# Four due times moved in a step loop over 64 chunks: sums of v, kb, an accumulating transfer, and T2 against KV

## The chip, the cores and the metric

The kernel runs on one core of a Trainium2 chip, in float32 throughout. The metric is the device time of one execution in microseconds (us); for a kernel that was run several times it is the median.

The engines are named as the profile names them: PE is TensorE (PEld its weight loads), DVE is VectorE, ACT is ScalarE, POOL is GpSimd, and SP is SyncE, which here only issues DMA transfers. GpSimd issues some transfers as well. Each engine works through its own list of instructions in order and waits on semaphores of the others.

## The reference

Input x has 8 images of 512 channels with 64 x 64 points. Two attention layers follow one another.

```
layer 0:  f = Wf x + bf                      (64 channels, 4096 points)
          g = maxpool2x2(Wg x + bg)          (64 channels, 1024 points)
          v = maxpool2x2(Wh x + bh)          (256 channels, 1024 points)
          beta = softmax(f^T g) over the 1024 points
          x = gamma * (Wv (v beta^T) + bv) + x
layer 1:  Q, K, V = wq x + bq, wk x + bk, wv x + bv      (64, 64, 512 channels)
          Qf, Kf = 10 relu(.) + exp(10 min(., 0))
          KV   = Kf V^T                                   (64 x 512)
          norm = 1 / (Qf . (sum of Kf over the points + eps))
          x = x + gamma * Qf KV * norm
```

## The kernel before, in words

An image is cut into 8 chunks of 512 points, so there are 64 chunks. The function `step(s)` is called for s from -9 to 64 and lays out what belongs to one step; j = s mod 8 is the place of chunk s in its image. A step with 0 <= s < 55 does four things side by side:

- For chunk a = s + 9 it makes f, g and v (`a_conv`). Three by four blocks of weights times four by two of x are multiplied in 20 products in place of 24, which asks for sums of blocks of x (GpSimd, tiles `v`, line 360) and for sums of the products' chains A to E out of PSUM (VectorE, tiles `h` and `fg`, line 377 and its neighbours). f goes through HBM and comes back later (`store_f`, `load_f`); v is pooled, turned and moved through HBM into `vT` (`flip_v`, `move_v`, `join_v`).
- For chunk s + 1 it makes the scores and their exponentials (`weigh`, tile `E`: TensorE `s`, line 616, ScalarE line 620), adds the exponentials over the 1024 points on VectorE (`sum_of_e`, tile `r`, lines 654 to 659), has TensorE finish these sums (`total`, tile `tot`, line 673), takes the reciprocals (line 683), spreads them over the partitions through HBM (`spread_inverses`: transfers `rd`, line 688, and `rb`, line 690), and multiplies E by them in four blocks (`normalize_block`, line 713).
- For chunk s it multiplies v with the normalized E (`attend`) and the result with Wv (`project`), each in seven products in place of eight. This asks for four sums of blocks of v (`sums_of_v`, tiles S1 to S4, once an image, lines 597 to 601), four sums of blocks of E (`sums_of_e`, tiles T1 to T4, lines 720 to 729) and sums behind the products. In `project` the results are added to x: either ScalarE copies a result out of PSUM and GpSimd adds it (`evict`, lines 812 and 815; `add_copy`, lines 823 and 824), or VectorE adds it from PSUM (`add`, line 818). Then x goes to HBM as the input of layer 1, its features are taken (`features`, tile `pk`, line 858), and it is turned (`flip_x`, `across`, `along`) so that K's features can be multiplied with it (`gather`, tile `pg`, summed in `G`).
- For the image before, b - 1, it finishes layer 1. In the step with j = 0, `start_kb` makes ksum and the matrix `kb` from the sums of K's features (lines 973 to 980, seven small VectorE operations), `normalize` multiplies Q's features with kb (`pd`, line 1067), inverts (line 1074) and spreads the result (`rn`), and `turn_G` turns G. In the step with j = 1, `make_KV` makes KV: TensorE `pkv` (line 1036), VectorE out of PSUM into `kv` (lines 1045 and 1049). In the steps with odd j, `finish` multiplies Q's features of a pair of chunks with KV (`pa`, line 1105), ScalarE copies the result to `y` (line 1108), and GpSimd issues two transfers of 1 MB each that add y onto the output in HBM (line 1111).

The order is written out by hand. Inside a step, `at(t, fn, ...)` puts an operation on a list with a due time t; the list is sorted by t, and the instructions are issued in this order. A due time is thus no time of the clock: it says only behind which other operations an instruction stands in its engine's list. VectorE, GpSimd, ScalarE, TensorE and SP each get their part of the one list.

Tiles are scarce. E, r, T1 to T4, S1 to S4 and `xb` have one buffer each, `y` has two, which are also used for the weights w_v1, and PSUM has eight banks. In a step with 0 <= s < 55 the banks of s, pa and pkv are taken in turn out of five (m3 to m7); most others are fixed.

The second half of the program repeats all of this with safer exponentials (`general=True`); it is only entered when a sum left the range, which does not happen with these inputs.

The lines that place what is changed (of the kernel before):

```python
if a % NCHUNK == 0:
    at(29.25 if early else 31.3, sums_of_v, (a - 1) // NCHUNK)
...
at(5.7 if a < TOTAL else 0.2, start_kb, b_c)
...
finish(pair, (2, 3), at, 32.4 if cover else t + 0.1, None if cover else 22.7 if a >= TOTAL else 8.206)
```

Of the kernel before, what the change touches and what calls it, by code (L numbers as in the profile page):

```python
# [8 lines left out]
F32 = mybir.dt.float32  # L9
AF = mybir.ActivationFunctionType  # L10
ALU = mybir.AluOpType
# [4 lines left out]
P = 128  # L16
# [6 lines left out]
def tile_two_attention_blocks(  # L23
# [21 lines left out]
    nc = tc.nc  # L45
# [6 lines left out]
    NCHUNK = N // CH  # L52
# [129 lines left out]
    def run(ctx, general):  # L182
# [402 lines left out]
                vT[:, 0:CV].rearrange("p (v q i) -> p v q i", v=VT, q=NT),  # L585
            )

        def sums_of_v(b):

            hm = MT // 2  # L590
            a11, a12, a21, a22 = (
                st[b]["vT"][:, bass.ts(j, hm), bass.ts(i, P)] for i in range(2) for j in range(2)
            )
            s1, s2, s3, s4 = (
                work1.tile([P, hm, P], F32, tag=f"S{i}", name=f"S{i}_{b}") for i in range(1, 5)
            )
            nc.gpsimd.tensor_tensor(s1, a21, a22, ALU.add)
            nc.gpsimd.tensor_tensor(s4, a11, a12, ALU.add)
            nc.gpsimd.tensor_tensor(s4, s1, s4, ALU.subtract)
            nc.gpsimd.tensor_tensor(s2, a11, s1, ALU.subtract)  # L600
            nc.gpsimd.tensor_tensor(s3, a11, a21, ALU.subtract)
            st[b]["v7"] = {1: a11, 2: a12, 3: s4, 4: a22, 5: s1, 6: s2, 7: s3}


# [175 lines left out]
        def project(s, at, t, t_store):  # L780
# [62 lines left out]
            at(t + t_evict[1], evict, (1, 1))  # L843
            at(t + (3.8 if last else 6.5), add, (0, 0), 2, ALU.add)
            at(t + t_add[0], add, (1, 0), 7, ALU.add)
            more = add if last else add_copy
            at(t + (t_add[1] if last else 3.41), more, (1, 0), 4, ALU.subtract)
            at(t + t_add[2], more, (1, 1), 7, ALU.add)
            at(t + t_add[3], add_rest)
            if s < TOTAL - 1:  # L850
                at(t_store, store)
# [363 lines left out]
        def step(s):  # L1215
# [10 lines left out]
            def at(t, fn, *args):  # L1226
                work.append((t, len(work), fn, args))
# [12 lines left out]
            if here:  # L1240
                ts = {
                    1: (0.0, None), 2: (1.7, 4.0), 3: (3.45, None), 6: (8.8, 10.7), 7: (10.5, 12.4),
                    4: (12.2, 14.1), 5: (13.85, 17.7),
                } if a <= TOTAL else {
                    1: (0.0, None), 2: (1.7, 4.0), 3: (3.9, None), 6: (14.4, 16.1), 7: (16.2, 17.9),
                    4: (17.9, 19.7), 5: (19.6, 22.5),
                }
                if s == 0:
                    ts.update({6: (4.0, 4.5), 7: (4.1, 4.6), 4: (4.2, 4.7), 5: (4.3, 4.8)})
                attend(s, at, ts)  # L1250
                if not (a <= TOTAL and s):
                    at(-0.6, sums_of_e, s, 3)
                at(5.6 if a <= TOTAL and s else 0.3, sums_of_e, s, 4)
                if a <= TOTAL and s:
                    at(-0.1, sums_of_e, s, 2)
            if 0 <= s - 1 < TOTAL:
                late_k = waits(s - 1)
                if late_k:
# [23 lines left out]
                if here:  # L1282
                    gather(s - 1, at, *((30.9, 32.6) if late_k else (14.3, 16.6) if a <= TOTAL else (12.6, 13.5)))
            if c_here and here and j == 0:
                at(5.7 if a < TOTAL else 0.2, start_kb, b_c)
                if a < TOTAL:
                    turn_G(b_c, at, (18.65, 18.75, 36.5))
                else:
                    turn_G_now(b_c, at, 19.5)
                if a >= TOTAL:  # L1290
                    make_KV(b_c, at, 21.4, 24.2, 24.2)
# [2 lines left out]
            if c_here and here and j == 1 and a <= TOTAL:  # L1294
                make_KV(b_c, at, 5.5, 5.55, 6.0)
            if c_here and here and j == 0:
                normalize(pair, at, 14.2 if a < TOTAL else 12.65, 15.95 if a < TOTAL else 13.7, 35.9 if a < TOTAL else 38.6)
            if c_here and here and j % 2 == 1 and j < NCHUNK - 1:
                normalize(pair + 1, at, 14.2 if a <= TOTAL else 12.65, 15.95 if a < TOTAL else 22.6 if a <= TOTAL else 13.7, 35.9 if a < TOTAL else 38.6)
            if c_here and here and j % 2 == 1:  # L1300

                cover = a == TOTAL
                t = 21.4 if cover else 9.2 if a > TOTAL else 8.0 if j == 1 else 3.6
                finish(pair, (0, 1), at, t, 24.9 if cover else 22.6 if a >= TOTAL else 8.15 if j == 1 else 3.75)
                finish(pair, (2, 3), at, 32.4 if cover else t + 0.1, None if cover else 22.7 if a >= TOTAL else 8.206)
            if 0 <= a < TOTAL:
                if a + 2 < LEAD - 1:
                    a_conv(a + 2)
# [13 lines left out]
            if 0 <= a - 1 < TOTAL:  # L1322
                early = a == NCHUNK
                if early:
                    at(29.2, a_turn, a - 1)
                else:
                    if ("pool", a - 1) in late:
                        at(6.9, late["pool", a - 1])
                    at(18.5 if not here else 6.95, flip_v, a - 1)
                    at(18.7 if not here else 7.0, move_v, a - 1)  # L1330
                    at(20.0 if not here else 22.0 if a % NCHUNK == 0 else 29.0, join_v, a - 1)
                if a % NCHUNK == 0:
                    at(29.25 if early else 31.3, sums_of_v, (a - 1) // NCHUNK)
            if s == -2:
                at(34.3, weigh_two, 0, 0)
                at(34.4, weigh_two, 0, 2)
# [3 lines left out]
            if after:  # L1340
# [25 lines left out]
                if not general:  # L1366
                    at(19.0 if t_invert == 15.9 and a < TOTAL else 26.0 if t_invert > 22 else 21.5, look, n)
                ts = {0: (28.3, 28.29, 33.5, 33.52), 1: (29.35, 29.4, 31.7, 31.8)}
                for i, t in zip((1, 0, 3, 2), ts.get(n, (36.6, 24.72, 29.2, 27.0) if a < TOTAL and c_here and j % 2 else (36.6, 24.0, 29.2, 25.2) if a < TOTAL else (24.3, 26.0, 27.3, 29.2))):
                    at(t, normalize_block, n, i // 2, i % 2)  # L1370
                at(36.606 if a < TOTAL and n else 33.6, sums_of_e, n, 1)
                if a < TOTAL and n:
# [144 lines left out]
```

## Time and profile before

| | |
|---|---|
| median of 3 runs | 2653.46 us (2651.44 to 2654.77) |
| the profiled execution, own time | 2651.42 us |
| its span, first to last instruction | 2649.6 us |
| PE, DVE, ACT, POOL busy | 97%, 81%, 55%, 53% |
| mean granted TensorE clock | 0.993 |
| DMA | 385.86 MB, 146 GB/s in the mean |

A step begins, in all that follows, with its first matmul of `M<-E,vT`; step 16 so begins at 736.25 us of the span and step 11 at 537.85. Steps 2 to 54 repeat in a pattern of eight. Those with even j other than 0 take 36.73 us in most cases; those with odd j take longer, since `pa` and `pd` come on top; the one with j = 1 has KV as well.

How to read the lines: a timeline's line has the start and the duration in us, the engine, the line of the kernel, the operation, output <- inputs with their shapes, the count, and in square brackets how long the engine stood idle before it and what released it. A line of the waits has the waiting instruction, what it waited for, then the total in us, the number of times and the longest. "PEclk" is the share of full speed that TensorE's clock was granted.

### The profile page before, as it was taken

The page shows a single profiled execution, that of the slowest core. Times are in us where ns is not written, and L with a number is a line of the kernel's source. Part 1 is how long each engine was busy: PE and PEld are TensorE (multiplying, and loading weights), DVE is VectorE, ACT ScalarE, POOL GpSimd, SP SyncE. Part 2 cuts the span into 40 slices and gives each one's busy share as a digit, 9 for nine tenths or more (in the row PEclk, how much of TensorE's full clock was granted, in tenths as well). Part 3 has the DMA queues.
Part 4 walks back from the last instruction along what each step waited for, and adds up shares of the span by engine and source line. Part 5 has one row for each costly group of instructions (what it writes and reads, how often), then busy time and mean ns, then how long its engine had stood idle before and what let it go on. Part 6 is the DMA issues. An engine that isn't in the chain of part 4 may idle for free.

```text
span 2649.6 us, 36263 instructions
## 1 busy us (share of the span) xinstructions
PE 2560.7 (97%) x11439; PEld 1847.3 (70%) x11439; DVE 2134.4 (81%) x3271; ACT 1456.1 (55%) x3300; POOL 1403.7 (53%) x1289
## 2 busy tenths in 40 slices
PE   9899999999999999999999999999999999989997
PEld 6677776777767777677776677677776677756664
DVE  6788888787788787888787887877887877878884
ACT  2255654665655665655655655656655556545553
POOL 5646556556556557556556556555556465421112
PEclk9999999999999999999999999999999999999999
DMA  6233443564554554644555545655545555444557
GB/s 181 80 102 118 140 135 121 153 169 131 152 158 128 159 164 129 173 129 137 164 145 156 156 124 140 181 138 157 149 124 165 151 149 154 126 125 126 139 138 261
DMA packets 271711, 385.86 MB, mean 146 GB/s; under 512 B 93404, under 2 KB 111768, under 8 KB 271512
## 3 DMA queue, kind: packets, MB, share of 16 engines
q1 hardware_dynamic: 254264, 323.94, 39.1%
q0 software_dynamic: 15232, 58.72, 11.6%
q8 instruction: 94, 1.54, 0.2%
q10 hardware_dynamic: 2016, 0.79, 0.1%
q14 instruction: 105, 0.86, 0.1%
HBM read 198.71 MB, written 150.04 MB: 132 GB/s over the span
## 4 chain that ended last, share of the span: by engine, by line
PE 72%; DVE 17%; issue 3%; SPq 3%; DMA 2%; ACT 1%; POOL 0%; DVEq 0%; ACTq 0%; POOLq 0%
PE M L741 24%; PE N L802 11%; PE s L616 7%; PE pk L858 6%; PE A L367 5%; PE pg L944 4%; PE pa L1105 4%; DVE E L713 3%; PE B L367 3%; SPq L1015 2%; PE C L367 2%; PE E L367 2%; DVE xf L907 2%; DVE h L377 1%; PE D L367 1%
## 5 line engine op out<-in xcount | busy, mean ns | idle before, releaser
L360 POOL TENSOR_TENSOR v<-xa 128x256 f32<-128x256 f32 x345 | 349.2, 1029 | 496.6 <-DMA xa<-in_x_dram 446.1
L815 POOL TENSOR_TENSOR xb<-xb,n 128x512 f32<-128x512 f32 x192 | 290.7, 1514 | 294.8 <-ACT n L812 294.0
L741 PE MATMUL M<-T,S 128*128 128x256 f32 x1536 | 359.0, 384 | 0.0
L360 POOL TENSOR_TENSOR v<-xa,v 128x256 f32<-128x256 f32 x410 | 346.5, 846 | 18.3
L741 PEld LDWEIGHTS M<-T,S 128*128 128x128 f32 x1536 | 287.1, 190 | 84.5 <-issue 31.7
L542 ACT COPY xT<-xf 32x512 f32<-32x512 f32 x504 | 310.1, 615 | 15.2 <-DVE xf L907 9.3
L713 DVE TENSOR_TENSOR E<-E,rb 128x1024 f32<-128x1024 f32 x220 | 310.4, 1412 | 0.0
L620 ACT ACTIVATE E<-s 128x512 f32<-128x512 f32 x512 | 263.4, 640 | 65.4 <-PE s L616 36.5
L616 PE MATMUL s<-f,g 64*128 64x512 f32 x1024 | 264.6, 621 | 10.7 <-DVE kv L1045 5.7
L1111 POOL DMA_DIRECT2D out_dram<-y x56 | 69.9, 1248 | 358.2 <-ACT y L1108 356.7
L802 PE MATMUL N<-to,w_v 128*128 128x256 f32 x1024 | 253.5, 382 | 4.6 <-ACT n L812 4.5
L741 PE MATMUL M<-E,vT 128*128 128x256 f32 x1024 | 234.0, 382 | 5.2 <-DVE E L713 2.6
L741 PEld LDWEIGHTS M<-E,vT 128*128 128x128 f32 x1024 | 195.7, 191 | 56.2 <-issue 29.4
L413 ACT ACTIVATE fs<-A,b_fg 64x256 f32<-64x256 f32 x62 | 29.1, 469 | 374.3 <-DVE fg L403 367.1
L858 PE MATMUL pk<-xb,w_kqk 128*128 128x512 f32 x512 | 232.7, 597 | 1.3 <-DVE xb L829 1.3
L812 ACT ACTIVATE n<-N,gb_v 128x256 f32<-128x256 f32 x384 | 159.9, 467 | 123.0 <-PE N L802 111.2
L802 PEld LDWEIGHTS N<-to,w_v 128*128 128x128 f32 x1024 | 195.2, 191 | 33.2 <-ACT n L812 6.9
L616 PEld LDWEIGHTS s<-f,g 64*128 64x128 f32 x1024 | 123.3, 186 | 122.0 <-issue 50.2
L824 POOL TENSOR_TENSOR xb<-xb,n 128x512 f32<-128x512 f32 x110 | 201.5, 1832 | 4.4
L367 PE MATMUL A<-v,w_p 128*128 128x256 f32 x620 | 184.8, 381 | 10.8 <-DVE fg L377 8.9
L802 PE MATMUL N<-o,w_v 128*128 128x256 f32 x768 | 188.1, 381 | 4.0 <-ACT tot L704 2.9
L656 DVE TENSOR_TENSOR r<-r,E 128x1024 f32<-128x1024 f32 x128 | 175.4, 1370 | 8.5 <-ACT E L620 0.9
(211 smaller groups left out, 4939.9 us busy)
## 6 DMA issues: line engine op xcount, KB each, us to landing
xb<-in_x_dram SPq DMA_DIRECT2D x64, 1024.0 KB
out_dram<-xb SPq DMA_DIRECT2D x63, 1024.0 KB
xa<-in_x_dram SPq DMA_DIRECT2D x59, 1024.0 KB
out_dram<-y POOLq DMA_DIRECT2D x56, 1024.0 KB, 11.5
xT<-xf SPq DMA_DIRECT2D x504, 64.0 KB
f<-fd SPq DMA_DIRECT2D x128, 128.0 KB
rb<-rd SPq DMA_DIRECT2D x55, 256.0 KB
fd<-fs SPq DMA_DIRECT2D x64, 128.0 KB
```

What stands on the lines that cost most here:

```text
L360: e.tensor_tensor(operand(to_), operand(x), operand(y), op)
L367: nc.tensor.matmul(rows_of(chains[c]), w_p[:, p - 1, :], operand(OPERAND[p]), start=p in HEADS, stop=True, skip_group_check=True,)
L542: nc.scalar.copy(to_, of)
L616: nc.tensor.matmul(sc[e], g[half(e), i, :], fs[s][half(e), :], start=True, stop=True)
L620: nc.scalar.activation(es[s][:, 2 * i + e, :], sc[e], AF.Exp)
L656: nc.vector.tensor_tensor(sums[s], sums[s], es[s][:, m : m + 2, :], ALU.add)
L713: nc.vector.tensor_tensor(b, b, r, ALU.mult)
L741: nc.tensor.matmul(a, v7[i][:, k, :], te[s][i][:, k, :], start=not more and k == 0, stop=k == hm - 1, skip_group_check=more,)
L802: nc.tensor.matmul(a[:, k, :], w_v7[i][:, bass.ts(k, P)], b, start=not more and k == 0, stop=True, skip_group_check=more or k > 0,)
L815: nc.gpsimd.tensor_tensor(of_x(*ij), of_x(*ij), u, ALU.add)
L824: nc.gpsimd.tensor_tensor(of_x(*ij), of_x(*ij), u, op)
L858: nc.tensor.matmul(pk, w_kqk[:, i, e * D : (e + 2) * D], x_b[s][:, i, :], start=(i == 0), stop=(i == KT - 1),)
```

## The change

It moves instructions in their engines' lists, splits one group and lets another engine do two sums. TensorE has the same matmuls; on its list only `pd` and `pg` change places, in the steps with j = 0 (s = 8 to 48). SP's list is the same.

- `sums_of_v` can be called in three parts: S3 and three quarters of S1; three quarters of S4 and S2; the last quarter of S1, S4 and S2. For every image but the first, the parts have the due times 19.8, 27.6 and 31.3 in the step before the image's (j = 7), where the whole had 31.3. On GpSimd, S3 and the first part of S1 now stand behind the ten first sums of blocks of x and ahead of the first sum into xb, the other parts behind the last sum into xb. There are nine instructions in place of five; for the first image all nine stand where the five stood.
- In `project`, in the steps with j = 7, the two `add_copy` (ScalarE copy and GpSimd sum) become `add` on VectorE. The first stands behind the first three sums of h and ahead of the first multiplication of E; the second, with a later due time, ahead of the third multiplication.
- `start_kb` (j = 0): from 5.7 to 13.15, that is from behind L729 to behind L659 and ahead of L766; on the way it passes the pooling of v (L422, L424, L557) and the sums of the exponentials. `normalize` of this step: its matmuls `pd` go from 14.2 to 16.55, behind `pg`; the reciprocal L1074 keeps its place between L683 and G.
- The second transfer of `finish` in steps with odd j: from 8.206 to 20.03. On GpSimd's list it stood behind the first two sums of blocks of x and now stands behind twelve of them and the first sum into xb, ahead of the `add_copy` sum (in j = 7 ahead of the next sum of blocks).
- `normalize_block` in the steps with odd j: the first block of E goes from 24.72 to 24.0 (ahead of two sums of fg and h), the second from 27.0 to 25.2 (ahead of a sum into xb and two sums of h), as they stand in the steps with even j.
- `sums_of_e` number 2 (T2, L723) in the steps with j = 1: from -0.1 to 5.56, behind L753 and KV (L1045, L1049).

```diff
-        def sums_of_v(b):
+        def sums_of_v(b, part=None):
...
-            s1, s2, s3, s4 = (
-                work1.tile([P, hm, P], F32, tag=f"S{i}", name=f"S{i}_{b}") for i in range(1, 5)
-            )
-            nc.gpsimd.tensor_tensor(s1, a21, a22, ALU.add)
-            nc.gpsimd.tensor_tensor(s4, a11, a12, ALU.add)
-            nc.gpsimd.tensor_tensor(s4, s1, s4, ALU.subtract)
-            nc.gpsimd.tensor_tensor(s2, a11, s1, ALU.subtract)
-            nc.gpsimd.tensor_tensor(s3, a11, a21, ALU.subtract)
+            if not part:
+                st[b]["S"] = [
+                    work1.tile([P, hm, P], F32, tag=f"S{i}", name=f"S{i}_{b}") for i in range(1, 5)
+                ]
+            s1, s2, s3, s4 = st[b]["S"]
+
+            def add(out, x, y, op, n):
+                nc.gpsimd.tensor_tensor(out[:, n], x[:, n], y[:, n], op)
+
+            if not part:
+                add(s3, a11, a21, ALU.subtract, slice(0, hm))
+            early, rest = slice(0, hm - 1), slice(hm - 1, hm)
+            for when, n in ((0, early), (2, rest)):
+                if part in (None, when):
+                    add(s1, a21, a22, ALU.add, n)
+                if part in (None, when + (when == 0)):
+                    add(s4, a11, a12, ALU.add, n)
+                    add(s4, s1, s4, ALU.subtract, n)
+                    add(s2, a11, s1, ALU.subtract, n)
...
-            more = add if last else add_copy
+            more = add if last or s % NCHUNK == NCHUNK - 1 else add_copy
             at(t + (t_add[1] if last else 3.41), more, (1, 0), 4, ALU.subtract)
-            at(t + t_add[2], more, (1, 1), 7, ALU.add)
+            at(t + (t_add[2] if last or more is add_copy else 10.1), more, (1, 1), 7, ALU.add)
...
-                    at(-0.1, sums_of_e, s, 2)
+                    at(5.56 if j == 1 and c_here else -0.1, sums_of_e, s, 2)
...
-                at(5.7 if a < TOTAL else 0.2, start_kb, b_c)
+                at(13.15 if a < TOTAL else 0.2, start_kb, b_c)
...
-                normalize(pair, at, 14.2 if a < TOTAL else 12.65, 15.95 if a < TOTAL else 13.7, 35.9 if a < TOTAL else 38.6)
+                normalize(pair, at, 16.55 if a < TOTAL else 12.65, 16.59 if a < TOTAL else 13.7, 35.9 if a < TOTAL else 38.6)
...
-                finish(pair, (2, 3), at, 32.4 if cover else t + 0.1, None if cover else 22.7 if a >= TOTAL else 8.206)
+                finish(pair, (2, 3), at, 32.4 if cover else t + 0.1, None if cover else 22.7 if a >= TOTAL else 20.03)
...
-                    at(29.25 if early else 31.3, sums_of_v, (a - 1) // NCHUNK)
+                    if early:
+                        at(29.25, sums_of_v, (a - 1) // NCHUNK)
+                    else:
+                        for t, i in ((19.8, 0), (27.6, 1), (31.3, 2)):
+                            at(t, sums_of_v, (a - 1) // NCHUNK, i)
...
-                for i, t in zip((1, 0, 3, 2), ts.get(n, (36.6, 24.72, 29.2, 27.0) if a < TOTAL and c_here and j % 2 else (36.6, 24.0, 29.2, 25.2) if a < TOTAL else (24.3, 26.0, 27.3, 29.2))):
+                for i, t in zip((1, 0, 3, 2), ts.get(n, (36.6, 24.0, 29.2, 25.2) if a < TOTAL else (24.3, 26.0, 27.3, 29.2))):
```

## The prediction

> **What bounds the kernel now.** Read first: the page's busy times, and its chain of work by engine.
>
> ```profile
> PE 2560.7 (97%) x11439; PEld 1847.3 (70%) x11439; DVE 2134.4 (81%) x3271; ACT 1456.1 (55%) x3300; POOL 1403.7 (53%) x1289
> ```
>
> TensorE is busy for 97%, and the change leaves its matmuls as they are. Only the 89 us in which it is not busy (2649.6 - 2560.7), and stretches at a lower clock, can be won. Second view: TensorE's waits.
>
> ```profile
> PE tot L673 <- DVE r L659: 19.2, 7, 3.4
> PE A L367 <- DVE h L377: 17.3, 26, 1.4
> ...
> PE s L616 <- DVE kv L1045: 5.7, 6, 1.0
> ```
>
> These three come by the kind of step. I count a step from its first `M<-E,vT` and write j for its place in its image (s mod 8). Third view: sums over single steps; these are s = 11, 12, 16 and 48 (j = 3, 4, 0, 0).
>
> ```profile
> 537.85:579.57 41.72, 41.06 (x190) 29.91 (x188) 32.45 (x49) 25.18 (x57) 25.07 (x22) 1.00 0.69 184
> 579.57:616.30 36.73, 36.73 (x165) 27.14 (x164) 31.39 (x50) 21.23 (x49) 20.64 (x19) 1.00 0.35 108
> 736.25:776.79 40.54, 37.72 (x173) 27.52 (x172) 36.38 (x58) 21.37 (x49) 27.36 (x23) 1.00 0.41 127
> 2020.43:2062.62 42.19, 39.38 (x174) 28.02 (x173) 36.52 (x58) 21.37 (x49) 27.15 (x23) 0.96 0.42 131
> ```
>
> First number the length, second TensorE's busy time, then the other engines', and the TensorE clock. An even step is bare matmul (36.73 = 36.73). An odd step stands idle 0.66, j = 0 2.82. The six with j = 0 last 43.11, 40.54, 40.53, 41.04, 40.55 and 42.19; the first and the last show a clock of 0.96. Fourth view: timelines. VectorE and TensorE around step 16 (starts at 736.25):
>
> ```profile
> 734.86 1.29 DVE L407 TENSOR_TENSOR g<-fg 64x128 f32<-64x128 f32 x1
> ...
> 738.58 2.32 DVE L713 TENSOR_TENSOR E<-E,rb 128x1024 f32<-128x1024 f32 x1
> ...
> 747.38 0.31 DVE L973 TENSOR_REDUCE kp<-ks 64x1 f32<-64x4 f32 x2
> ...
> 755.12 0.88 DVE L659 TENSOR_TENSOR r<-r 128x512 f32<-128x512 f32 x1
> ...
> 756.06 0.43 PE L673 MATMUL tot<-r,ones 128*32 128x128 f32 x8 [2.82 <-DVE r L659]
> ```
>
> VectorE runs without a gap until L659, which TensorE awaits. Two of its rows are long (2.32 against 1.18 to 1.22 elsewhere, 1.29 against 0.29): they stood behind GpSimd's sums of v. And kb's seven operations (L973 to L980) stand in the line.
>
> **The change, part by part.** Sum against the profiled execution: 2651.42 us (span 2649.6, 1.8 around it), 2.0 under the median of 2653.46.
>
> *kb behind the sums (j = 0 of images 1 to 6: s = 8, 16, ..., 48).* Seven operations, from 747.38 to 748.79, leave VectorE's line ahead of L659: 1.41 a step. They now stand ahead of L766; what waits for them there is L767 (o for the projection) and L683 (reciprocal). VectorE has 2.9 us idle later in this step (27.38, before h<-h,E), so 1.41 fits. If that cover were gone, the projection would start 1.41 late. pd goes behind pg, 2 us later, so that kb is done in time; its reciprocal follows L683 anyway.
>
> *Sums of v.* Before, five of 1.27 us (6.35) run on GpSimd from 3.5 us ahead of the step's end into the next step's 3.6. After: one whole and one of three quarters in GpSimd's idle time before its first xb sum (23 to 26.7 us; TensorE has finished with S by 20.2), and the rest, three of 384 columns and four of 128, at the end. From 256 columns at 0.72 and 512 at 1.27 I take 384 at 1.0 and 128 at 0.45: 3 + 1.8 us. Two GpSimd sums of 1.27 (L824) also go, to VectorE as two L818 of 0.67 that read PSUM. GpSimd so ends near the step's end, and the 2.32 becomes about 1.2. Against that VectorE has 1.34 more in this step. I take 0.75 of net lead at the start of j = 0. Bounds: 0 (the L818 eat it) and 2.1 (both long rows go).
>
> So L659 ends 2.16 earlier, TensorE waits 0.7 instead of 2.8: 6 x 2.16 = 13.0; s = 8 and 32 have 0.6 and 0.5 more wait to lose: 14.1. In steps 8 and 48 a stretch of 3.41 us at half clock follows the wait; each costs 1.65 (42.19 against 40.54 at equal waits, 2.81 and 2.82). With waits of 0.7 I expect none: 3.3. Together 17.4. The Trainium skill (TensorE: Matmul & The Clock Gate, Part 1: The HAM clock gate) lets the clock fall only after about 3.4 us without work; by that rule step 48 would not have slowed, and the 1.65 there is not this wait's: 15.8 in place of 17.4. The row shows 2.81 to be enough at times, and I stay with it.
>
> *Second accumulating transfer (23 steps with odd j, s = 9 to 53).* Now step 11:
>
> ```profile
> 559.47 0.55 SPq L688 DMA_DIRECT2D rd<-rq  x1
> 564.63 0.36 SPq L690 DMA_DIRECT2D rb<-rd  x1
> ...
> 575.17 0.70 PE L367 MATMUL A<-xa,w_p 128*128 128x256 f32 x2 [0.66 <-DVE h L377]
> ```
>
> The transfer issued at 553.73 (L1111) is in flight while rd and rb go (5.16 us between their issues, in even steps 1.7), so the first multiplication of E is placed two VectorE sums later than in even steps and the rest of the line presses against `A`. After, the transfer is issued some 14 us later, behind the v sums; rb then takes the even steps' 1.7 and E stands as in even steps, which have no wait. Without its wait step 11 would be 40.87 (A could start 0.43 behind D, at 574.34, not 575.17): 0.83 each. What is moved past: the issue holds GpSimd's queue for 0.78 (to the next start), now in front of L824, two v sums and three xb sums. By the rows, L824 for (1,1) then ends about 39.2 in the step instead of 38.0, where pk's third block needs it at about 39.1: I charge 0.15. And qq<-qq,rn (L1087) lands on L407, as it does at the end of step 16 (L407 1.29); VectorE enters the next, even step 0.4 later, where L659 ends 0 to 0.5 ahead of need: 0.25. Net for j = 1, 3, 5: 18 x (0.83 - 0.15 - 0.25) = 7.7. Bounds 0 and 18 x 0.83 = 14.9. The moved 1 MB meets rn, the vT transfers and the 1 MB store; its landing (8.3 to 13.7 us) reaches the store's time, and nothing waits for either before 7 us into the next step.
>
> A rule against this part: the Trainium skill (SBUF — State Buffer, Who interferes with whom) says that a transfer issued from GpSimd can lack its descriptors while VectorE holds the shared port pair, and gives 620 ns becoming 3100. As an estimate from that page, 2.5 us more on GpSimd's queue, and so on pk, would make this part 23 x (0.83 - 2.5) = -38 in place of +7.7. The 56 issues here took 1.19 to 1.66, some of them beside VectorE's tensor_tensor, and I keep the row's 0.78.
>
> *j = 7.* Here the two L818 come in the same line ahead of `A`: of 0.83 I keep 0.4 in five steps (2.0), and s = 7, which has no wait now, loses 0.2. Bounds -0.5 and 0.83 each. New waits: GpSimd's second xb sum waits for the first L818; the second L818 waits for GpSimd's third xb sum, and behind it on VectorE stand a multiplication of E, two h sums and L403, for which ScalarE's fs waits. That sum ends about 1.4 before it is asked for.
>
> *T2 behind KV (j = 1, six steps).* Step 17, from 776.79:
>
> ```profile
> 786.89 1.99 PE L616 MATMUL s<-f,g 64*128 64x512 f32 x8 [0.95 <-DVE kv L1045]
> ...
> 788.51 2.06 ACT L620 ACTIVATE E<-s 128x512 f32<-128x512 f32 x4 [0.91 <-DVE T L729]
> ```
>
> KV (1.3 us) passes L723 (1.2), so the 0.95 in front of s goes. But pa needs the banks that ScalarE's second four exponentials free, those wait for T4 (L729), and T4 comes after the same VectorE work in either order. The wait moves to pa: gain 0 (bounds 0 and 6 x 0.95 = 5.7).
>
> Sum: 17.4 + 7.7 + 2.0 - 0.2 = 26.9. 2651.4 - 26.9 = 2624.5 in the profiled execution, 2626.5 on the median's scale.
>
> **Rivals.** (a) *All waits go*: j = 0 falls to 36.73 + 0.23 (pd) = 36.96, or 26.2 in six steps; odd ones 23 x 0.83 = 19.1. 2653.5 - 45.3 = 2608; with KV 2602. For it: even steps show the same order with no wait. Against: even steps keep at most 0.5 us of slack at L659. (b) *Only kb counts*: 6 x 1.41 + 1.65 = 10, and the GpSimd/VectorE collisions only change places: 2643. For it: every long row above is such a collision. (c) *Slower*: GpSimd's line is the place. If the 0.78 of the issue costs one more lost turn at the port (1.25), L824 ends 1.4 late for pk and L407 holds up the next step by 1.2: 23 x 2.6 = 60 against 17.4 + 19.1 = 36.5 gained, 2677. It decides from 36.5 / 23 = 1.6 us per odd step on. Against: GpSimd is idle 3.2 us before its first xb sum and starts the rest on time. (d) *The edits hit nothing*: excluded for kb, whose 1.41 stands in the line that TensorE awaits.
>
> **How the numbers follow.** Forecast 0.56, (a) 0.14, (b) 0.18, (c) 0.12. (a) and (b) are faster as well, (b) with a tail into no change. 0.2% (5.3 us) is about what a measurement of this kernel tells from none. Faster 0.86, same 0.04, slower 0.10. Range 2608 to 2646: (a) at one end, (b) with its tail at the other.
>
> **What would show it.** tot <- r from 19.2 to about 6 us, no half clock after steps 8 and 48; s <- kv gone, with waits of pa <- ACT in its place and j = 1 at about 44.3; rb issued under 2 us after rd in odd steps, A <- h near 2 us; odd steps at 40.9 to 41.1, even ones at 36.7 to 37.0, with small waits for L659; L407 at 1.29 in most odd steps. Wrong if pk waits for L824, if rb still comes late (E then blocks the chains' sums), or if j = 0 keeps over 1.5 us at tot.

## The result: 3.1% slower

The changed kernel takes 2736.14 us in the median of four runs (2734.19 to 2738.45); beside it the kernel before took 2654.11 (four runs, 2651.44 to 2655.19). The ratio is 1.0311, with a 95% interval of 1.0293 to 1.0329. The forecast was 2626.5, with a range that ended at 2646.

In the profiled execution the span is 2736.7 us, 87.1 more than before. Cut into steps and summed by their place j (before, after, us):

| steps | before | after | difference |
|---|---|---|---|
| j = 0 (six steps) | 247.95 | 240.68 | -7.27 |
| j = 1 (six) | 270.14 | 301.30 | +31.16 |
| j = 3 (six) | 250.29 | 280.89 | +30.60 |
| j = 5 (six) | 250.29 | 281.10 | +30.81 |
| j = 7 (five) | 207.48 | 208.75 | +1.27 |
| j = 2, 4, 6 (eighteen) | 662.19 | 661.19 | -1.00 |
| up to step 7, and from step 55 on | 761.30 | 762.75 | +1.45 |

So the steps with j = 1, 3 and 5 lose 92.6 us, 5.14 each; all else together wins 5.5. In these 18 steps the second accumulating transfer and the first two multiplications of E were moved. Both were moved in the steps with j = 7 as well, which lose only 0.25 each; there the sum behind the transfer's issue is another one, since the two block sums went to VectorE, and the sum after that starts only 0.03 us ahead of its end (step 15: 739.37 against 737.69 + 1.71).

First line of the page of after, on busy times:

```profile
PE 2601.9 (95%) x11439; PEld 1873.5 (68%) x11439; DVE 2218.3 (81%) x3283; ACT 1448.3 (53%) x3288; POOL 1360.4 (50%) x1309
```

TensorE has the same 11439 matmuls, but is busy 41.2 us longer, and not busy for 134.8 us (2736.7 - 2601.9) instead of 88.9. Both halves of the loss are there: 45.9 us more of waiting, and 41.2 us more for the same matmuls, with a mean granted clock of 0.977 in place of 0.993. Next, TensorE's waits after the change, and the costliest group of VectorE:

```profile
PE A L367 <- DVE h L377: 70.0, 27, 3.5
PE C L367 <- DVE to L782: 9.7, 6, 1.8
...
PE pa L1116 <- ACT E L631: 4.1, 6, 0.7
...
PE tot L684 <- DVE r L670: 3.4, 6, 1.2
```

```profile
L724 DVE TENSOR_TENSOR E<-E,rb 128x1024 f32<-128x1024 f32 x220 | 381.6, 1735 | 0.0
```

The waits for r and for KV, at which the change aimed, have gone or moved as forecast (`tot` from 19.2 to 3.4 us, `s <- kv` replaced by 0.7 at `pa`). But `A <- h`, which was to fall, rose from 17.3 to 70.0 us, and a wait of chain C is new. The multiplication of E (L724, L713 before) takes 1735 ns in the mean (1412 before). Then single steps, in the same columns as before; these are steps 11, 12, 16 and 48, and step 13 in the third line:

```profile
540.35:586.57 46.22, 42.72 (x189) 31.06 (x188) 37.29 (x51) 25.18 (x57) 23.77 (x22) 0.96 0.64 167
586.57:623.31 36.74, 36.74 (x166) 27.13 (x165) 30.31 (x48) 21.21 (x49) 20.69 (x19) 1.00 0.34 107
623.31:670.85 47.54, 44.06 (x190) 32.03 (x189) 37.36 (x51) 25.18 (x57) 23.71 (x22) 0.93 0.62 162
749.31:789.53 40.22, 38.14 (x174) 27.49 (x172) 36.27 (x59) 21.47 (x50) 21.85 (x20) 1.00 0.40 126
2091.88:2132.06 40.18, 38.12 (x173) 27.48 (x172) 36.24 (x59) 21.47 (x50) 21.85 (x20) 1.00 0.41 127
```

Step 11 now stands idle 3.50 us (0.66 before) and its clock is 0.96, in step 13 0.93: after such a wait come 3.4 or 6.8 us of matmuls at half clock. Steps 16 and 48 are both at full clock. Last, timelines: step 11 from 540.35, and step 16 from 749.31 (engine SPq is SyncE's queue):

```profile
561.97 0.55 SPq L699 DMA_DIRECT2D rd<-rq  x1
563.60 0.36 SPq L701 DMA_DIRECT2D rb<-rd  x1
...
569.91 1.18 POOL L1122 DMA_DIRECT2D out_dram<-y  x1
...
570.68 1.71 POOL L835 TENSOR_TENSOR xb<-xb,n 128x512 f32<-128x512 f32 x1
...
571.77 5.50 DVE L724 TENSOR_TENSOR E<-E,rb 128x1024 f32<-128x1024 f32 x1
...
572.14 0.93 POOL L360 TENSOR_TENSOR v<-xa,v 128x256 f32<-128x256 f32 x1
...
572.83 1.47 POOL L826 TENSOR_TENSOR xb<-xb,n 128x512 f32<-128x512 f32 x1
...
574.05 0.92 POOL L360 TENSOR_TENSOR v<-xa,v 128x256 f32<-128x256 f32 x1
574.74 1.45 POOL L826 TENSOR_TENSOR xb<-xb,n 128x512 f32<-128x512 f32 x1
576.26 2.15 POOL L835 TENSOR_TENSOR xb<-xb,n 128x512 f32<-128x512 f32 x1
577.20 0.67 DVE L829 TENSOR_TENSOR xb<-xb,N 128x512 f32<-128x512 f32 x1
...
578.36 0.47 PE L367 MATMUL A<-v,w_p 128*128 128x256 f32 x1 [3.50 <-DVE h L377]
...
766.75 0.42 PE L684 MATMUL tot<-r,ones 128*32 128x128 f32 x8 [0.48 <-DVE r L670]
...
767.50 1.33 DVE L991 TENSOR_SCALAR kb<-ones,ksum 64x64 f32<-64x64 f32 x2
...
770.65 0.89 DVE L1085 RECIPROCAL rq_pd<-pd 128x128 f32<-128x128 f32 x1
...
772.01 0.41 DVE L782 TENSOR_TENSOR to<-M,m 128x256 f32<-128x256 f32 x1
...
772.56 0.67 PE L367 MATMUL C<-v,w_p 128*128 128x256 f32 x2 [1.57 <-DVE to L782]
```

The reader is to see four things. rb now goes 1.6 us after rd, so the aim of the transfer's move was reached. The transfer's issue (L1122, 569.91) is followed by the xb sum 0.77 later, before the issue's own row has ended; and from there on every GpSimd sum starts 0.2 to 0.3 us before the one ahead of it has ended (572.14 against 570.68 + 1.71 = 572.39, and so on). The second multiplication of E is given to VectorE at 571.77 and ends at 577.27: 5.50 us in place of about 1.2. It ends 1.08 us after the first pause in GpSimd's row (574.74 + 1.45 = 576.19; the next starts at 576.26). Behind it stand the sums of h that chain A waits for. And in step 16, tot waits 0.48 in place of 2.82, but chain C waits 1.57 for L782, ahead of which kb's seven operations now stand (pd's reciprocal stood there before as well).

### The profile page after: what moved, and what is told of

Same layout as the page of the kernel before. It is cut to its first block, busy times and chain, and to the rows that moved or that the text cites. A ratio compares the mean times of both kernels' runs of the same rounds, so it can differ in the third digit from the quotient of the medians.

```text
span 2736.7 us, 36250 instructions
## 1 busy us (share of the span) xinstructions
PE 2601.9 (95%) x11439; PEld 1873.5 (68%) x11439; DVE 2218.3 (81%) x3283; ACT 1448.3 (53%) x3288; POOL 1360.4 (50%) x1309
## 4 chain that ended last, share of the span: by engine, by line
PE 77%; DVE 15%; issue 5%; ACT 1%; DMA 1%; POOL 0%; DVEq 0%; SPq 0%; ACTq 0%; POOLq 0%
PE M L752 25%; PE N L813 10%; PE s L627 8%; PE pk L869 7%; PE A L367 6%; PE pg L955 4%; PE pa L1116 4%; DVE E L724 4%; PE B L367 4%; PE C L367 3%; PE D L367 3%; DVE h L377 2%; PE E L367 2%; DVE xb L829 1%; DVE xf L918 1%
## 5 line engine op out<-in xcount | busy, mean ns | idle before, releaser
L826 POOL TENSOR_TENSOR xb<-xb,n 128x512 f32<-128x512 f32 x192 | 251.7, 1311 | 314.9 <-ACT n L823 313.3
L724 DVE TENSOR_TENSOR E<-E,rb 128x1024 f32<-128x1024 f32 x220 | 381.6, 1735 | 0.0
L360 POOL TENSOR_TENSOR v<-xa,v 128x256 f32<-128x256 f32 x410 | 362.9, 886 | 18.3
L367 PE MATMUL A<-v,w_p 128*128 128x256 f32 x620 | 197.9, 404 | 78.5 <-DVE h L377 69.6
L1122 POOL DMA_DIRECT2D out_dram<-y x56 | 66.7, 1191 | 339.6 <-ACT y L1119 338.0
L835 POOL TENSOR_TENSOR xb<-xb,n 128x512 f32<-128x512 f32 x98 | 207.8, 2121 | 3.9
L367 PEld LDWEIGHTS A<-v,w_p 128*128 128x128 f32 x620 | 120.7, 200 | 105.7 <-issue 70.2
```

Source lines behind the costliest of these rows:

```text
L360: e.tensor_tensor(operand(to_), operand(x), operand(y), op)
L367: nc.tensor.matmul(rows_of(chains[c]), w_p[:, p - 1, :], operand(OPERAND[p]), start=p in HEADS, stop=True, skip_group_check=True,)
L724: nc.vector.tensor_tensor(b, b, r, ALU.mult)
L826: nc.gpsimd.tensor_tensor(of_x(*ij), of_x(*ij), u, ALU.add)
L835: nc.gpsimd.tensor_tensor(of_x(*ij), of_x(*ij), u, op)
```

## The experiments

Times are medians; each ratio is against runs of the kernel before on the same chip. A "long row" is a multiplication of E that takes more than 2.4 us in the timeline. VectorE "gets in" at the end of a GpSimd sum when a multiplication of E that was pending then runs next; otherwise it is "passed over".

### Which part loses the time

The second transfer and the order of E were moved in the same steps. The theory after the result was that the transfer's issue, right ahead of GpSimd's sums, keeps VectorE waiting; its rival, that the new order of E does so by itself. Four kernels take them apart.

**Transfer back**, all else as changed:

```diff
-finish(pair, (2, 3), at, ..., 20.03)
+finish(pair, (2, 3), at, ..., 8.206)
```

> The changed kernel, with the second accumulating transfer back at its old due time (8.206); all else as changed, E's multiplications at 24.0 and 25.2 too. Theory P (the transfer's issue right ahead of GpSimd's sums into xb is what leaves VectorE's second multiplication of E without its turn for 5.5 us): no row of L724 over 2.4 us, the wait of 3.5 us for h in j = 1, 3, 5 gone, 2633 to 2648 us. Theory R (the earlier place of the second multiplication alone makes it collide with GpSimd's row of sums): the rows of 5.5 us stay, about 2735 us.

Measured: 2652.11 us, ratio 1.000 (0.999 to 1.001). No row of the multiplication of E is above 2.4 us. The 84 us are gone with the transfer alone, so the order of E does not make them. The time is some 4 us above what was expected, and VectorE's group says why:

```profile
L724 DVE TENSOR_TENSOR E<-E,rb 128x1024 f32<-128x1024 f32 x220 | 323.7, 1472 | 15.4 <-DMA rb<-rd 15.4
```

With the transfer in its old place rb is late again, and E, placed earlier, now waits for it (15.4 us in all). The steps with j = 3 and 5 come out at 40.87 to 42.43, one at 44.32.

**Transfer and E back**: the four due times of E in odd steps go back to 36.6, 24.72, 29.2, 27.0 as well.

> The changed kernel, with the second transfer and E's multiplications in odd steps back where they were: only sums of v, kb, the two L818 of j = 7 and T2 behind KV are left of the change. Both theories: no long rows. The steps with j = 0 keep the 7.3 us in all that they won, the rest loses 1 to 2: 2645 to 2651 us, 5 us under the kernel before.

Measured: 2642.13 us, ratio 0.9965 (0.9951 to 0.9979), better than expected. The rest of the change (kb, sums of v, the j = 7 sums, T2) is worth 9 to 10 us, and the steps with j = 0 account for all of it (237.28 against 247.95). Against the kernel with the transfer alone put back only the order of E differs: with the transfer in its old place, the earlier E costs 10 us.

**Transfer alone**, put into the kernel before:

> The kernel before, with nothing but the second transfer moved to 20.03 (E's multiplications where they were). Theory P: a multiplication of E still stands behind GpSimd's row after the issue, with rows over 4 us, 2700 to 2750 us. Theory R: no long rows, 2645 to 2655 us.

```diff
-finish(pair, (2, 3), at, ..., 8.206)
+finish(pair, (2, 3), at, ..., 20.03)
```

Measured: 2765.19 us, ratio 1.0429 (1.0411 to 1.0446), worse than either theory had it. All 23 odd steps now have a row of 5.5 us, those with j = 7 too; with the old order it is the first multiplication of E that is held up.

```profile
PE A L367 <- DVE h L377: 93.6, 35, 3.5
PE tot L673 <- DVE r L659: 13.7, 7, 3.4
```

**Transfer and E together**, put into the kernel before (due times of E as in even steps):

> The kernel before, with the second transfer at 20.03 and E's multiplications as in the changed kernel; sums of v, kb, j = 7 and KV as before. Both theories: the rows of 5.5 us in j = 1, 3, 5 are all there, and the loss of 92 us with them: 2740 to 2755 us. If the loss is under 60 us, the other parts of the change have a share in it.

Measured: 2753.45 us, ratio 1.0380 (1.0363 to 1.0398). All 23 odd steps have a row of 5.5 us again. The order of E alone as the cause has fallen: whatever multiplication of E stands at that place in VectorE's list is held up, if the transfer stands where the change put it.

### What it is about the transfer

Two explanations were left. Either the transfer itself, its packets or descriptors, keeps VectorE off (its packets now run from 31 to 37 us in step 11; before, those of the step's two transfers ran from 13 to 26); or its issue sets GpSimd's next sums so close to one another that VectorE never gets its turn ("no pause, no turn").

**A dependent small operation** of GpSimd, right behind the sum that follows the issue, so that GpSimd must wait for its own result:

```diff
+if ij == (1, 0) and NCHUNK <= s < TOTAL - LEAD and s % 2:
+    w = small.tile([P, 1], F32, tag="gap", name=f"gap_{s}")
+    nc.gpsimd.tensor_tensor(w, x_b[s][:, 2, 0:1], x_b[s][:, 2, 0:1], ALU.add)
```

> The changed kernel with one addition: in the odd steps 9 to 53, right behind the GpSimd operation of the block sums (L835) that follows the second accumulating transfer's issue, a 128x1 GpSimd addition that reads what that operation has just written. GpSimd must then wait for its own result before it goes on. Theory gap (the issue makes each of the next five GpSimd operations start before its predecessor has ended, so that GpSimd never lets go of the memory port it shares with VectorE, and VectorE's second multiplication of E gets in only at the first gap): the 5.5 us row falls to at most about 2.6 us, TensorE's 3.5 us wait in these steps to 1 us or less and its half clock is gone: 2.8 to 5.2 us in each of 18 steps back, 2640 to 2690 us. Theory data (the transfer's own packets or descriptors, which move from 31 to 37 us in these steps, hold VectorE off): the row stays at 5.5 us and the time at 2730 to 2740 us.

Measured: 2640.49 us, ratio 0.9955 (0.9939 to 0.9972). The transfer is issued and lands as in the changed kernel (29.57 and 38.12 us into step 11; there 29.56 and 38.11), yet no row is above 2.4 us. One more instruction on GpSimd gives back some 92 us (82.0 above before, 9.7 below). This excludes the transfer's data.

**The same operation on a constant**, without the wait:

```diff
-    nc.gpsimd.tensor_tensor(w, x_b[s][:, 2, 0:1], x_b[s][:, 2, 0:1], ALU.add)
+    nc.gpsimd.tensor_tensor(w, two[:, 0:1], two[:, 0:1], ALU.add)
```

> The control to the run with the dependent 128x1 addition: the same addition at the same place, but it reads a constant, so GpSimd has nothing to wait for. Theory gap: the row stays near 5.5 us, since the stream of GpSimd operations has no gap, and the time at 2730 to 2745 us. Theory data: the same, 2730 to 2745 us. If the time falls as much as with the dependent one, it is not the wait for the result but one more instruction that lets VectorE in.

Measured: 2648.74 us over ten runs from 2636.41 to 2657.90, ratio 0.9988 (0.9970 to 1.0005). Both theories had said 2730 or more, and both missed. Of the 18 steps with j = 1, 3 and 5 of the profiled execution 17 have no long row, one has (step 35, 5.66). The other nine runs were not profiled; how many long rows they had is open. The timeline of step 11, one of the 17:

```profile
562.78 1.19 POOL L1125 DMA_DIRECT2D out_dram<-y  x1
563.56 1.71 POOL L835 TENSOR_TENSOR xb<-xb,n 128x512 f32<-128x512 f32 x1
565.02 1.38 POOL L838 TENSOR_TENSOR gap<-two 128x1 f32<-128x1 f32 x1
565.17 1.91 POOL L360 TENSOR_TENSOR v<-xa,v 128x256 f32<-128x256 f32 x1
...
564.65 1.72 DVE L724 TENSOR_TENSOR E<-E,rb 128x1024 f32<-128x1024 f32 x1
```

(GpSimd's rows first, then VectorE's.) The small operation starts 0.25 us ahead of the end of the sum before it (565.02 against 565.27), as close as the v sum in the changed kernel. Still VectorE gets in when that sum ends: its 1.72 end at 566.37, 1.10 later, and now the small operation waits (1.38). So it takes no wait for a result; a one-element operation in the row is enough in most steps, not in all. The theory "no pause, no turn" is thereby too narrow: this row is as close as that of the changed kernel, and VectorE gets in.

**The transfer later**, due at 36.0, behind GpSimd's last sum of the step, where it has nothing more to do:

> The changed kernel with the second accumulating transfer due at 36.0 in steps j = 1, 3, 5 in place of 20.03: behind the block sums and the last GpSimd operation of the step, where GpSimd has nothing to do. Theory gap: no GpSimd operation follows the issue closely, so no 5.5 us row, and rb's issue still goes early: 2620 to 2640 us. Theory data: the packets then run in the first 10 us of the next even step, and whatever VectorE does there (the evictions of the projection) is held off instead: above 2700 us.

Measured: 2642.98 us, ratio 0.9968 (0.9957 to 0.9979). No long row; the steps with j = 3 and 5 take 40.86 or 40.87. The packets now run at the start of the next step, and the even steps get small new waits there (`D <- POOL v` 3.2 us in all, `A <- h` 5.4): 37.6 us in place of 36.7, some 16 us in the 18 steps, which is more than the miss of 3 us.

**The transfer one place earlier**, due at 19.85: ahead of the first xb sum, for which GpSimd has to wait anyway:

> The changed kernel with the second accumulating transfer due at 19.85 in place of 20.03 in steps j = 1, 3, 5: one place earlier on GpSimd's queue, ahead of the first block sum that waits for its operand. Theory gap: GpSimd waits after the issue, the stream is broken, no 5.5 us row: 2620 to 2645 us. Theory data: the packets still run beside the second multiplication of E: the row stays long, above 2700 us.

Measured: 2637.94 us, ratio 0.9946 (0.9929 to 0.9963). Step 11 of this kernel, the windows and the timeline:

```profile
533.86:574.73 40.87, 40.87 (x190) 29.78 (x189) 32.34 (x48) 25.18 (x57) 25.90 (x22) 1.00 0.69 171
```

```profile
563.45 2.25 POOL L835 TENSOR_TENSOR xb<-xb,n 128x512 f32<-128x512 f32 x1
565.65 1.71 POOL L360 TENSOR_TENSOR v<-xa,v 128x256 f32<-128x256 f32 x1
567.32 1.27 POOL L826 TENSOR_TENSOR xb<-xb,n 128x512 f32<-128x512 f32 x1
...
565.28 1.49 DVE L724 TENSOR_TENSOR E<-E,rb 128x1024 f32<-128x1024 f32 x1
```

No wait, full clock: 40.87 us, 0.85 less than before the change. The v sum starts only 0.05 us ahead of the end of the sum before it (565.65 against 565.70), and VectorE gets in at that end (565.28 + 1.49 = 566.77, 1.07 later). All steps with j = 3 and 5 take 40.87. Place against place, one position of one DMA issue is worth some 94 us (82.0 above its own runs of before, 12.3 below them).

Three odd steps of this kernel are still disturbed. In step 17 (47.78) rb is issued 2.6 us after rd in place of 1.6. In steps 23 and 39, of j = 7 (44.44 and 43.05), a multiplication of E takes 4.12 and 3.77 us. In j = 7 the first part of the early sums of v stands right ahead of the transfer, and GpSimd no longer waits behind the issue, where it waits 2.5 us in step 11.

Whether the 0.05 and the 0.25 are the difference can be counted. I took every end of a GpSimd sum at which a multiplication of E was pending, in fourteen traces (before, after, and all experiments but the one with the constant operand), from step 3 on. Where the next GpSimd sum had started 0.13 us or less ahead of that end, or later, VectorE got in at 1752 of 1775 such ends (its row ended within 1.35 us). Where the next had started more than 0.13 us ahead, it got in at 0 of 282. In 22 of the 23 misses of the first kind the multiplication had come less than 0.04 us ahead of the end. The limit of 0.13 was read off these same counts. Steps 15 and 39 of the last kernel show it with the same instructions in the same order: in step 15 the next sum starts 0.10 us ahead of an end and VectorE gets in there (its row takes 1.78 us); in step 39 it starts 0.19 ahead of the same end, and VectorE is passed over (3.77).

The control with the constant has 17 of 22 beyond the limit, 17 of 18 where the small operation is the next one: it is an exception to this count. That a close row of full sums keeps VectorE out is thus shown by the count and by the experiments; why it does, and why the small operation lets VectorE in, is not settled by these runs.

### The other parts, with the transfer out of the way

All of these start from the kernel with the transfer due at 19.85 (2637.94; its j = 0 steps sum to 237.08, 39.5 each, chain C's wait is 1.58).

**kb back** in its old place:

```diff
-at(13.15 ..., start_kb, b_c)
+at(5.7 ..., start_kb, b_c)
-normalize(pair, at, 16.55 ..., 16.59 ..., 35.9 ...)
+normalize(pair, at, 14.2 ..., 15.95 ..., 35.9 ...)
```

> The changed kernel with the second accumulating transfer due at 19.85 (no long row), and kb's operations with pd's product and reciprocal put back to their old places (5.7, 14.2, 15.95): of j = 0's two parts only the sums of v are left. Theory cover (the move of kb put 2.2 us of kb's operations and pd's 0.9 us reciprocal ahead of L782, which chain C's head waits for through the bank it shares with M5): the 1.58 us wait of chain C goes and 1.4 us of kb's operations stand ahead of r again, so that tot waits 1.4 to 1.7 us: a j = 0 step takes 39.3 to 40.0 us against 39.5 on average with both, 2630 to 2640 us. Theory of the prediction (each of the two parts saves its own time): 1.4 us more in each of six steps, 2643 to 2648 us.

Measured: 2637.15 us, ratio 0.9945 (0.9928 to 0.9961). j = 0 takes 39.9 in the mean, chain C's wait is gone, tot waits 1.8 to 2.0 us. By these steps moving kb is worth at most 0.4 us a step, not 1.41: it exchanges one wait for another. The profiled execution was the slowest of the four (2643.55, the others 2635.45 to 2637.53), and the medians (2637.15 against 2637.94) show no gain at all. Two of its j = 0 steps, s = 24 and s = 40:

```profile
1054.80:1093.67 38.87, 37.02 (x173) 27.27 (x172) 34.72 (x57) 21.37 (x49) 22.85 (x20) 1.00 0.43 136
1694.75:1735.32 40.57, 38.72 (x174) 27.54 (x172) 34.70 (x57) 21.36 (x49) 22.70 (x20) 0.96 0.43 136
```

Both wait 1.85 us for r. One goes on at full clock, the other has its `pg` matmuls at 1061 ns in place of 592 (half clock) and loses 1.70 us.

**Sums of v back**, all nine instructions at 31.3:

```diff
-for t, i in ((19.8, 0), (27.6, 1), (31.3, 2)):
-    at(t, sums_of_v, (a - 1) // NCHUNK, i)
+at(31.3, sums_of_v, (a - 1) // NCHUNK)
```

> The changed kernel with the second accumulating transfer due at 19.85, and all of GpSimd's sums of v back behind the last step of the image (due 31.3): of j = 0's two parts only kb's move is left. Theory cover: r's chain ends 2.1 us later and everything behind it with it, so that tot waits 2.2 to 2.6 us and chain C still 1.6 us: a j = 0 step takes 41.3 to 42 us, or 43 to 45 where half clock follows the wait, 2647 to 2665 us. Theory of the prediction: tot's wait is 2.82 - 1.41 = 1.4 us, no wait at chain C: 39 us, 2634 to 2640 us.

Measured: 2635.25 us, ratio 0.9942 (0.9925 to 0.9958). The time is the one that the prediction's theory gave, but not for its reason: tot waits 0.3 to 0.6 us, chain C 1.57 to 1.77, j = 0 39.7. The early sums of v bring 0.2 us a step in j = 0 (39.5 against 39.7) and cost more in j = 7: with them back at the end the long rows of steps 23 and 39 are gone, and all five steps take 40.98 or 40.99 (204.9 in all against 210.7).

**Block sums back too**: from there, the two block sums of j = 7 return from VectorE to GpSimd.

```diff
-more = add if last or s % NCHUNK == NCHUNK - 1 else add_copy
+more = add if last else add_copy
```

> The run with the sums of v back, and the j = 7 edit taken back as well: two of the block sums return from VectorE to GpSimd. Kb's move, the E order and the transfer (due 19.85) stay. Theory queue (it is these two sums, and not the place of the sums of v, that let GpSimd end earlier and so give VectorE its lead at the start of j = 0): GpSimd's sums of v end about 2.5 us later, VectorE's chain 1.3 us later, tot waits 1.6 to 2.2 us in place of 0.3 to 0.6, and j = 0 takes 40.5 to 41.5 us: 2640 to 2648 us. Rival (the lead comes from kb's move and the E order alone): tot stays at 0.3 to 0.6 us and the time at 2634 to 2638 us.

Measured: 2649.72 us, ratio 0.9994 (0.9984 to 1.0004). The 14 us are back, a little above the expected range, and at another place than expected:

```profile
PE M L752 <- POOL S L601: 18.8, 6, 3.1
```

GpSimd's sums of v end at 8.4 us in the j = 0 step, and TensorE waits for S itself, 3.13 us in each of the six, and a stretch of half clock follows each time (43.0 a step). So with the sums at the end, it is the two block sums that hold them up. Whether the early sums of v alone, without the j = 7 edit, would have sufficed was not run.

**pd's reciprocal behind L783** (from 16.59 to 17.75), sums of v as changed:

> The changed kernel with the second accumulating transfer due at 19.85, and pd's reciprocal (L1085, 0.89 us) due at 17.75 in place of 16.59, behind L782 and L783. Theory cover: chain C's wait falls from 1.58 to about 0.7 us, 0.9 us in each of six steps, 2630 to 2635 us. Rival (chain C waits for something else than the place of L782 behind those operations): 1.58 us as before, 2636 to 2640 us.

Measured: 2636.02 us, ratio 0.9944 (0.9927 to 0.9961). Chain C's wait falls from 1.58 to 0.74 to 0.95, as the place of L782 in VectorE's list demands; of the 0.8 us, 0.6 are left in the step (38.9), some of the rest in tot's wait (7.2 us in all in place of 5.4). It is at the edge of what the medians can tell.

**Together**: transfer at 19.85 (36.0 for j = 1, where rb once came late beside it), the reciprocal behind L783, the sums of v back.

> Four things together: the changed kernel with the second accumulating transfer due at 19.85 for j = 3 and 5 and at 36.0 for j = 1 (where rb once came late beside it), pd's reciprocal behind L783 (17.75), and all sums of v behind the image's last step, as before the change. From the profiled run with the sums of v back (span 2633.2): 0.85 us less at chain C in six steps (5.1), and the single late rb of step 17 gone (3.5): 2626 to 2632 us. If the gains do not add up: 2633 to 2637 us.

Measured: 2628.73 us, four runs from 2628.37 to 2629.34, ratio 0.9912 (0.9897 to 0.9928). Better than both kernels: 22.1 us under its runs of before, and some 104 under the changed kernel (22.1 + 82.0). Its waits:

```profile
PE C L367 <- DVE to L782: 4.7, 6, 0.9
PE tot L684 <- DVE r L670: 4.5, 13, 1.2
PE A L367 <- DVE h L377: 4.4, 13, 1.4
PE pa L1116 <- ACT E L631: 4.1, 6, 0.7
```

## Why the prediction was wrong

**The step that failed** is the second accumulating transfer, "the issue holds GpSimd's queue for 0.78 (to the next start) ... I charge 0.15", with bounds of 0 and +14.9. The gap to the next start was right (0.77). The cost lay elsewhere: behind the issue GpSimd's sums follow one another so closely that VectorE's second multiplication of E is passed over at four ends in a row and takes 5.50 us (step 11). TensorE waits 2.8 us longer, and loses 2.3 more to the half clock: 5.14 in each of 18 steps, 92.6 us in place of a gain of 7.7. Rival (c) had the place (GpSimd's line and the port), and came nearer with its 2677, but had the wrong loser: it charged a lost turn to GpSimd and pk, and VectorE was the one that lost its turns. Rows of 2.3 us, in which VectorE waited out one sum of GpSimd's, were in the profile of before; that it could be several in a row, with half clock behind, was in no bound and in no rival, and no row of before showed it.

**The rule that was set aside.** The Trainium skill (SBUF — State Buffer, Who interferes with whom) warns that GpSimd's transfer can wait for VectorE. That did not happen: the issue took 1.18 us in step 11, no more than before (1.20), and the transfer landed 8.6 us later. So it was right to set this aside as a price. The same section puts this harm on VectorE's two-port modes and says that `tensor_tensor`, which VectorE runs beside the issue in step 11, has none, so the -38 was worked out for a case that the page does not describe. The harm here went the other way: behind the transfer's issue VectorE had to wait. The same page (SBUF: two separate sides) says that an operation of VectorE with two inputs from memory, or one of GpSimd, whichever starts first, gets the shared pair of ports for its whole instruction, and the other is blocked so long. The traces agree for the 1752 ends; in the rows with the 282 others the block lasted not for one instruction but for up to five.

**rb and the order of E**: right. rb went 1.6 us after rd, and with the transfer one place earlier the steps with j = 3 and 5 take 40.87, the 0.83 of the working (41.72 - 40.87 = 0.85). The even steps pay 0.3 each of that back, 0.25 had been charged.

**kb behind the sums**: the 1.41 did leave the line ahead of r, but the claim "VectorE has 2.9 us idle later in this step, so 1.41 fits" failed. The idle time lies behind L782, and chain C's first matmul waits for L782, since both use one PSUM bank (`HEADS` gives chain C's first product, 8, bank 6; `M5` has bank 6 as well). The seven operations also took 2.2 us in the new place (two of 64x64 took 0.64 and 0.68 us in place of 0.25, beside GpSimd's sums). Worth 0.4 a step at most, not 1.41.

**Sums of v**: the lead of VectorE was forecast (0.75 a step), and tot's wait did fall to 0.48; but the place of the sums of v was not needed for it in the runs: with the two block sums off GpSimd, tot waits no more than 0.6 us with the sums of v at the end as well. I had entered the block sums as a mere by-product, with VectorE's cost against them. The half clock behind steps 8 and 48 went, as said (3.3 us). In all, j = 0 won 7.3 us in place of 17.4; of the 10.1 missing, chain C's new waits are 9.7.

**j = 7**: +0.25 a step in the changed kernel in place of -0.4, with a wait of 0.93 for h; 41.08, so -0.4, in three of the five steps with the transfer one place earlier; the other two have the rows of about 4 us. Step 7 lost 0.53 (37.26 against 36.73), where 0.2 was charged.

**T2 behind KV**: right. `s <- kv` went, and 0.69 at `pa <- ACT E` took its place. Where neither the transfer nor E was moved, the step takes 45.17 against 45.03 before, so the gain of 0 held; the step with the transfer one place earlier takes 44.33 (44.3 forecast).

## What to carry to other kernels

When a DMA issue on GpSimd's queue is moved, look at what VectorE does with two inputs from memory in the next 6 us: put the issue ahead of an instruction for which GpSimd has to wait anyway, or at the end of its work, not ahead of a dense row of sums; and check that the wait is still there after the other edits (in j = 7 it was not). When operations are moved out of the way of one wait, list everything that comes behind their new place, PSUM banks that have to come free included, before the saving is booked. And bound a wait's cost together with the half clock that can follow it.

## What was not expected of the hardware

- One VectorE instruction of about 1.2 us was held up by 4.3 us over five GpSimd instructions. What told the cases apart was how long before the end of a GpSimd sum the next one starts: 0.13 us or less, 1752 of 1775 got in; more, 0 of 282; a GpSimd operation of one element per partition in the row let it in at 17 of 18.
- Half clock followed waits of 1.85 us as well as of 3.5, and waits of the same 1.85 us (steps 24 and 40 above) were followed by it or not. Where it came in step 40, it covered the narrow `pg` matmuls behind the wait.
- What decided was where the wait fell. In each of the fifteen traces half clock begins only at whole multiples of 3.413 us from the first such stretch. Cut steps 2 to 54 of all traces into windows on this grid, and take those at full clock: with up to 1.84 us of idle TensorE in a window the next was at half clock in 0 of 9118 cases, with more than 2.005 us in 71 of 71, between the two in 7 of 12. The 1.85 us of step 40 lay in one window; those of step 24 were shared by two (0.74 and 1.11). So the 3.4 us without work, by the rule that the prediction sets beside its sum, were not needed here.
- Two 64x64 operations of VectorE took 0.66 us in the mean where GpSimd's sums ran beside them, in six steps of after, and 0.25 where none did, before and after.
